# A four-layer transformer on one core: the order of a many-headed expert stage, a second routing's roots on ScalarE, and two moves at the seam of the first routing

## The chip, the cores and the metric

The kernel runs on one core of one Trainium2 chip. The metric is the device time of one execution in microseconds (us). A core has a matrix engine (PE; its weight loads are listed apart as PEld), a vector engine (DVE), a scalar engine (ACT, which evaluates functions from loaded tables), a general engine (POOL), and a queue that only starts transfers (SP). Each works through its own instruction queue in order, and they wait for each other on semaphores.

## The reference

`x` has 32 sequences of 256 rows with 128 features, 8192 rows in all. Four layers follow each other; each has an attention half and a feed-forward half, and each half is preceded by a layer norm and a modulation that depends on the sequence:

```
h = _layernorm(x, axis=-1) * (1 + ca) + sa
x = x + ga * attn(h)
h = _layernorm(x, axis=-1) * (1 + cb) + sb
x = x + gb * ffn(h)
```

The attention halves are a two-branch selective scan (layer 0), a local attention with Haar-level linear attention called "hale" (layer 1), an attention with phase windows (layer 2) and an attention over a latent of 32 (layer 3). The feed-forward halves that matter here are the first three:

```
# layer 0: a shared expert for every row, and 2 of 8 routed experts
shared = new_gelu(xf @ Wfc_s + bfc_s) @ Wproj_s + bproj_s
topk_p, topk_i = jax.lax.top_k(softmax(xf @ Wr), 2)     # then normalised
routed = sum over e of gate[:, e] * (new_gelu(xf @ Wfc[e] + bfc[e]) @ Wproj[e] + bproj[e])
# layer 1: 2 of 8 experts of 512 places each, filled in the order of the rows
logits = jax.nn.relu(x @ rw1 + rb1) @ rw2 + rb2
pos = jnp.cumsum(one_hot(ids), axis=0) - 1              # place of each row in its expert
disp[ids, pos] += x * (pos < CAP);  y = expert_out[ids, pos] * probs * keep
# layer 2: each of 8 heads (16 features) of each row picks 2 of 16 experts
h = x @ Wm + bm;  t = h.reshape(-1, 16);  w = softmax(t @ expert_emb)
hmid = gelu(einsum('td,edi->tei', t, W1) + b1);  eo = einsum('tei,eio->teo', hmid, W2) + b2
out = (sum of the two chosen eo, weighted by w) @ Wo + bo
```

The last feed-forward half quantizes its operands to FP4.

## The kernel before

`x` stays in the core's memory as 16 tiles of 512 rows, features on the partitions, rows along the free dimension. Eight stages run one after the other, each a method with its own pools of buffers (`pools`: a name and how many buffers it rotates through): `scan_layer`, `dense_moe` (L1009), `hale` (L1616), `capacity_moe` (L2076), `phase_attention`, `head_moe` (L2376), `latent_attention`, `fp4_mlp`. A buffer of a new stage lies in memory that an old stage's buffers had, and its first writer waits for their last readers.

**How the order is written.** Each stage fills an agenda: `put(t, f, ...)` enters a piece of work at step `t`, and the pieces are then called in order of `t`, those of one step in the order in which they were put. `mm` and `tr` (L398, L401) always pin the matmuls and transposes to that order, `act` (L405) pins ScalarE's where `strict_act` is set, and `nc.vector.on` pins VectorE's (by the wrapper `InOrder`, so that L310 is the profile's line for all of these). Whatever is not pinned is placed by the framework's scheduler. Matmul lines in the profile are L399, transposes L403, activations L406.

**dense_moe** (first routing). Tile `b` starts at step 4b: norm, rows `h`, logits, choice of 2 of 8 (`choose`), places, `scatter` (L1130: eight indirect transfers on POOL that put the tile's rows into the experts' regions in DRAM), gates (`route_gates`). 24 steps later `shared_part` (L1150, four pieces) computes the shared expert for this tile on PE and ACT and adds it to `x`. `route_totals` is at step 72, and 39 blocks of 512 routed rows follow, four steps each: `block_fetch` (weights `wts` and rows `dk` gathered by POOL), `block_turn` (four transposes `tp<-dk`), `block_hidden`, `block_out` (a copy `eo` by DVE, a store to `expert_rows` by SP). SP also issues the load of stage 7's weights, into the buffer that this stage's weights had, when the last reader of these is through.

**hale**. Its prelude makes constants: on POOL memsets of zeros and ones (`mts`, `vzb`, `vzl` at L1629 to L1632, `kvs` at L1639), on the other engines small weights. Then `hale_slots` runs an agenda whose first pieces, for each tile of 512, gather the routed rows that belong to it (`gather_rows`, L1294: two indirect transfers `got` on POOL for each of four row groups), sum them (`gather_sum`, `gy`) and add them to `x` (`gather_end`); norm and attention follow.

**capacity_moe** (second routing). Tile `b` starts at step 4b: `norm_stats` (transposes to PSUM, BATCH_NORM on DVE), `norm_apply` one step later, `norm_out` (rows `h`, transposed back), `router_hidden` (four matmuls and Relu), `router_sums` (logits `lT`, rows `ht`), `router_choice` (`choose`: two maxima with one-hots, `both`, then four running sums `past` and `seen`), `capacity_slots` (PE counts from `both` and `past`, DVE places, `scatter`). Only PE's order is pinned. With `newton` set, `norm_apply` takes 1/sqrt(v + eps) by integer shift and four Newton steps, all on DVE:

```
nc.vector.tensor_scalar(g, v.bitcast(I32), 1, None, ALU.arith_shift_right)
nc.vector.tensor_scalar(g, g, -1.0, float(0x5F3759DF), ALU.mult, ALU.add)
# four times: t = -0.5*y*y;  t = t*v;  y = (t + 1.5)*y
```

`rsqrt` (L413) is the other way: Ln and Exp on ACT and one refinement of four instructions on DVE. The weights and a zeroing of `disp` are issued as transfers at the start of the stage, part of them on ACT's queue.

**head_moe** (many-headed experts). A tile has 16 steps, one for each expert `e`: `moe_spread` (a transfer on SP that spreads the gate's row, `gb`), `moe_hidden` (four matmuls `S<-hm`, two Gelu of 128x1024 on ACT), and two steps later `moe_outputs` (four matmuls `po<-hid`, `ye = po * gb` on DVE, `acc += ye` on POOL). Between these the next tile is prepared: norm in three pieces (`moe_norm`, then Newton on DVE in two halves), rows (`moe_h`: transposes `tp<-ln_xn`, `h` on ACT), projection (`moe_heads`: `tp<-h,bigw`, `hm`), logits, choice, the exponential (`moe_exp`, with a table load before and after it), gates, `moe_turn`, `moe_bias`. All engines are pinned. In a step every `moe_hidden` is called first, then all other work. PSUM has three buffers for `S`, one for `po`, one for `tp`.

Of the kernel before, what the change touches and what calls it, by code (L numbers as in the profile page):

```python
# [30 lines left out]
P = 128  # L31
# [291 lines left out]
class Program:  # L323
# [129 lines left out]
    def norm_rows(self, src, small=None, tag="ln_xn"):  # L453

        nc = self.nc
        ps = self.ps("tp", (P, 4, P))
        for t in range(4):
            self.tr(ps[:, t, :], src[:, t * P : (t + 1) * P])
        xn = self.wk(tag, (P, 4, P))
        self.act(xn, ps, AF.Copy)  # L460
        st, mv, v = self.wk("ln_st", (P, 4, 6)), self.wk("ln_mv", (P, 4, 2)), self.wk("ln_v", (P, 4))
        for t in range(4):
            nc.vector.bn_stats(st[:, t, :], xn[:, t, :])
        for t in range(4):
            nc.vector.bn_aggr(mv[:, t, :], st[:, t, :])
        (small or nc.vector).tensor_scalar(v, mv[:, :, 1], 1e-5, None, ALU.add)
        return xn, mv, v

    def norm_place(self, xn, mv, v):
# [539 lines left out]
    def dense_moe(self, w):  # L1009
# [8 lines left out]
        with ExitStack() as ctx:  # L1018
# [19 lines left out]
            def put(t, f, *args):  # L1038
                agenda.setdefault(t, []).append((f, args))

            for b in range(NB):
                a = {"b": b}
                T = 4 * b
                put(T + 1, lambda a: a.update(xn=self.norm_apply(*a["st"])), a)
                put(T + 0, lambda a: a.update(st=self.norm_stats(self.x[a["b"]])), a)
                put(T + 3, lambda a: a.update(h=self.norm_out(a["xn"], self.ada_mods(0, 1, a["b"]), "h")), a)
                put(T + 5, self.route_logits, m, a)
                put(T + 10, self.route_slots, m, a)
                put(T + 13, self.route_gates, m, a)
                for i in range(4):  # L1050
                    put(T + 24 + i, self.shared_part, m, a, i)
            end = 4 * NB + 8
# [563 lines left out]
    def hale(self, w):  # L1616
        nc, c = self.nc, self.c
        BF = mybir.dt.bfloat16
        with ExitStack() as ctx:
# [8 lines left out]
            self.vzl = [keep.tile([P, 4, 16, 32], F, name=f"vzl{t}") for t in (0, 1)]  # L1628
            for t in self.mts + self.vzb + self.vzl:  # L1629
                nc.gpsimd.memset(t, 0.0)  # L1630
            for t in self.vzb + self.vzl:
                nc.gpsimd.memset(t[:, :, :, 8:16], 1.0)  # L1632
            self.identb = wk("identb", (P, P), BF)
# [4 lines left out]
            self.kvs = wk("kvs", (P, 5, SEQ))  # L1638
            nc.gpsimd.memset(self.kvs, 0.0)  # L1639
            self.kt = wk("kt", (P, 5, P))  # L1640
# [19 lines left out]
            self.gather = None  # L1660

    def hale_slots(self, w):

# [6 lines left out]

        tiles = {}
        for q in range(2 * NB):
            b, s = divmod(q, 2)
# [402 lines left out]
    def capacity_moe(self, w):  # L2076
# [3 lines left out]
        with ExitStack() as ctx:  # L2080
# [6 lines left out]
            self.pools(ctx, {"tp": 2, "hid": 3, "o": 1, "s": 2}, zero=1, ht=4, dk=4, hid=3, eo=3, h=3)  # L2087
            self.strict = self.newton = True
            zero = self.wk("zero", (P, 8 * P))
# [11 lines left out]
            def put(t, f, *args):  # L2101
                agenda.setdefault(t, []).append((f, args))

            for b in range(NB):
                a = {"b": b}
                T = 4 * b
                put(T + 1, lambda a: a.update(xn=self.norm_apply(*a["st"])), a)
                put(T + 0, lambda a: a.update(st=self.norm_stats(self.x[a["b"]])), a)
# [15 lines left out]
            for t in sorted(agenda):  # L2124
                for f, args in agenda[t]:
                    f(*args)
            self.strict = self.newton = False
            self.gather = {"eo": eo, "rows": 8 * CAP}
# [247 lines left out]
    def head_moe(self, w):  # L2376
# [5 lines left out]
        with ExitStack() as ctx:  # L2382
            w = self.load_pieces(ctx, "s5", [(x, None) for x in ("Wm", "bm", "emb", "b2", "b1", "w1", "w2", "Wo", "bo")])
            self.pools(ctx, {"S": 3, "po": 1, "tp": 1}, hid=6, gb=8, ye=3, hm=3, ln_xn=1)
            self.strict = self.strict_act = nc.vector.on = True
# [5 lines left out]
            for b in range(NB):  # L2391
                a = {"b": b}
                T = 16 * b
                put(T - 32, lambda a=a: self.moe_norm(a))
                for t in (-31, -30):
                    put(T + t, lambda a=a: next(a["norm"]))
                put(T - 28, lambda a=a: self.moe_h(a))
                put(T - 27, lambda a=a: self.moe_heads(w, a))
                put(T - 24, lambda a=a: self.moe_logits(w, a))
# [7 lines left out]
                for e in range(16):  # L2407
                    put(T + e - 3, lambda a=a, e=e: self.moe_spread(a, e))
                    put(T + e, (lambda a=a, e=e: self.moe_hidden(w, a, e), None))
                    put(T + e + 2, lambda a=a, e=e: self.moe_outputs(w, a, e))  # L2410
                put(T + 22, lambda a=a: self.moe_end(w, a))
            for t in sorted(agenda):
                works = agenda[t]
                for work in works:
                    if isinstance(work, tuple):
                        work[0]()
                for work in works:
                    if not isinstance(work, tuple):
                        work()
            self.strict = self.strict_act = nc.vector.on = False  # L2420
# [451 lines left out]
```

## Time and profile before

The kernel before took 6519.52 us (median of four runs, 6490.41 to 6537.06). One execution was profiled:

| | |
|---|---|
| profiled execution | 6520.15 us |
| its span | 6518.3 us, 132602 instructions |
| mean granted PE clock | 0.94 of full speed |
| busy: PE, PEld | 5750.6 us (88%), 3278.6 us (50%) |
| busy: DVE, ACT, POOL | 4205.6 (65%), 3472.7 (53%), 2855.7 (44%) |
| dense_moe | about 1055 to 1634 us of the span |
| hale | 1634 to 3683 |
| capacity_moe | 3683 to about 4042 |
| head_moe | about 4760 to 5520 |

A line of the timeline gives the start, the time from start to end, the engine, the code line, the operation, what it writes `<-` what it reads, and in brackets the idle time of the engine before it with what ended it. A line of the waits gives the waiting engine and what it was about to do, the instruction that it waited for, then the sum, the number and the longest of these waits. A line of the windows gives busy time and instructions of each engine, the granted PE clock, the share of the DMA engines that was busy, and the bytes moved. Busy shares over the whole span mix stages with different limits, so each edit is looked at in its own stretch.

### The profile page before, as it was taken

To read this page: it belongs to the slowest core of one execution; us is meant where nothing else is said; L and a number is where in the kernel's file an instruction comes from. 1 tells how busy PE (TensorE), PEld (TensorE's weight loads), DVE (VectorE), ACT (ScalarE), POOL (GpSimd) and SP (SyncE) were. 2 spreads that over 40 slices of the span, in tenths; PEclk is the share of its full clock that TensorE was granted. 3 is DMA by queue.
4 is the path that set the end of the run, shared out by engine and by line. 5 is a ranking of instruction groups with operands and counts; after the bars stand their busy time and mean duration, and the time that the engine had idled before them with its cause. 6 is when DMAs were issued, how large, how long until landed. Compare 5 with 4: busy or idle time off the path is not lost. (4 is left out here: it accounts for less than half of the span.)

```text
span 6518.3 us, 132602 instructions
## 1 busy us (share of the span) xinstructions
PE 5750.6 (88%) x54369; PEld 3278.6 (50%) x54369; DVE 4205.6 (65%) x9329; ACT 3472.7 (53%) x5045; POOL 2855.7 (44%) x3202
## 2 busy tenths in 40 slices
PE   6888886999899999999999776999979998999987
PEld 4666664466455555555555433455522222455544
DVE  4777776611466666666665562888767774677678
ACT  5888884333344444444444331444458887555532
POOL 4565553565444544444444353444334545222200
PEclk7999997999899999999999877999989999999988
DMA  2110111145000000000000101111034443000010
GB/s 63 42 43 35 37 42 38 48 118 125 16 6 5 7 6 5 6 6 5 7 3 2 48 1 36 24 29 29 24 82 90 92 91 75 14 20 20 19 35 30
DMA packets 175875, 232.17 MB, mean 36 GB/s; under 512 B 46567, under 2 KB 95967, under 8 KB 175010
## 3 DMA queue, kind: packets, MB, share of 16 engines
q1 hardware_dynamic: 124880, 126.50, 7.6%
q0 software_dynamic: 26992, 56.62, 3.7%
q10 hardware_dynamic: 23394, 40.58, 1.7%
q8 instruction: 427, 7.00, 0.5%
q14 instruction: 182, 1.49, 0.1%
HBM read 88.21 MB, written 74.97 MB: 25 GB/s over the span
## 5 line engine op out<-in xcount | busy, mean ns | idle before, releaser
L310 DVE TENSOR_REDUCE mt<-S 128x4 f32<-128x1024 f32 (+2 forms) x768 | 755.0, 998 | 534.0 <-PE S L399 530.6
L1471 ACT ACTIVATE E<-S 128x1024 f32<-128x1024 f32 x448 | 457.8, 1022 | 426.6 <-PE S L399 384.7
L910 DVE TENSOR_TENSOR_SCAN hs<-decay,dB 128x512 f32<-128x512 f32 x512 | 583.2, 1204 | 153.1 <-PE dB L399 113.8
L1962 POOL TENSOR_SCALAR_AFFINE_SELECT E<-E 128x1024 f32<-128x1024 f32 x320 | 348.7, 1092 | 584.3 <-ACT E L1961 583.9
L406 ACT ACTIVATE hid<-S,bigw 128x1024 f32<-128x1024 f32 x512 | 537.2, 1111 | 121.6 <-PE S L399 121.2
L310 DVE TENSOR_TENSOR E<-S,cst 128x1024 f32<-128x1024 f32 x320 | 391.1, 1222 | 289.3 <-PE S L399 289.2
L399 PE MATMUL S<-qa,kx 32*128 32x256 f32 x4096 | 510.9, 371 | 12.0 <-DVE mt L310 11.5
L399 PE MATMUL S<-kx,q 32*128 32x512 f32 (+1 forms) x2048 | 509.4, 591 | 3.0 <-POOL kx L1607 2.7
L2509 POOL TENSOR_TENSOR acc<-acc,ye 128x512 f32<-128x512 f32 x256 | 344.4, 1345 | 359.2 <-DVE ye L310 316.2
L1961 ACT COPY E<-S 128x1024 f32<-128x1024 f32 x320 | 323.5, 1011 | 325.3 <-PE S L399 313.5
L399 PE MATMUL S<-qG,f 32*128 32x512 f32 x2560 | 367.6, 644 | 47.4 <-DVE E L310 47.4
L399 PEld LDWEIGHTS S<-qa,kx 32*128 32x128 f32 x4096 | 325.9, 185 | 97.2 <-DVE mt L310 64.4
L403 PE MATMUL hT<-cst,hs 128*128 128x128 f32 x2048 | 298.8, 292 | 72.0 <-ACT hsT L406 68.1
L399 PE MATMUL S<-hm,bigw 32*128 32x512 f32 x2048 | 336.8, 649 | 24.9 <-ACT hid L406 24.9
L406 ACT ACTIVATE decay<-dl,A 128x510 f32<-128x510 f32 x512 | 338.5, 712 | 0.0
L406 ACT ACTIVATE hsT<-hT 128x1024 f32<-128x1024 f32 x256 | 259.7, 1015 | 122.3 <-PE hT L403 122.0
L399 PE MATMUL po<-hid,bigw 128*32 128x512 f32 x2048 | 277.9, 615 | 30.4 <-DVE ye L310 30.4
L403 PEld LDWEIGHTS hT<-cst,hs 128*128 128x128 f32 x2048 | 235.3, 148 | 124.7 <-ACT hsT L406 107.7
L1837 ACT ACTIVATE E<-S 128x768 f32<-128x768 f32 (+1 forms) x192 | 169.0, 880 | 237.7 <-PE S L399 237.5
L310 DVE TENSOR_TENSOR ye<-po,gb 128x512 f32<-128x512 f32 x256 | 175.9, 687 | 173.8 <-PE po L399 104.5
L399 PE MATMUL po<-E,vz 128*32 128x256 f32 x4096 | 287.1, 364 | 0.3 <-ACT oc L1491 0.2
L399 PE MATMUL po<-E,vzl 128*32 128x128 f32 x8192 | 276.8, 276 | 0.0
(540 smaller groups left out, 12985.4 us busy)
## 6 DMA issues: line engine op xcount, KB each, us to landing
gb<-gT SPq DMA_DIRECT2D x256, 256.0 KB
regions<-zeros ACTq DMA_DIRECT2D x16, 2048.0 KB
rx<-far SPq DMA_DIRECT2D x64, 256.0 KB
expert_rows<-eo SPq DMA_DIRECT2D x39, 256.0 KB
xin<-in_x SPq DMA_DIRECT2D x16, 256.0 KB
out<-out SPq DMA_DIRECT2D x16, 256.0 KB
xTd<-xT SPq DMA_DIRECT2D x15, 256.0 KB
xT<-xTd SPq DMA_DIRECT2D x15, 256.0 KB
```

The lines of the kernel that those rows point to most:

```text
L310: return lambda *args, **kw: self.tc.keep_in_program_order(op(*args, **kw))
L399: return self.tc.keep_in_program_order(self.nc.tensor.matmul(out, lhsT, rhs, start=start, stop=stop, **kw))
L403: return self.tc.keep_in_program_order(self.nc.tensor.transpose(out, in_, self.c.ident[:k, :k]))
L406: ins = self.nc.scalar.activation(*args, **kw)
L910: nc.vector.tensor_tensor_scan(hs[:, :, n], decay, dB[:, :, n], 0.0, ALU.mult, ALU.add)
L1471: nc.scalar.activation(e, src, AF.Exp, scale=scale)
L1837: nc.scalar.activation(e, src, AF.Exp, scale=1.0 / math.sqrt(8))
L1961: nc.scalar.copy(e, src)
L1962: nc.gpsimd.affine_select(e, e, [[0, 8], [1, P]], ALU.is_ge, 0.0, base=0, channel_multiplier=-1)
L2509: nc.gpsimd.tensor_tensor(a["acc"], a["acc"], ye, ALU.add)
```

## The change

Four edits. (A) In `dense_moe` the shared parts of tiles 9, 10 and 11 are put at the steps behind the last expert block. (B) In `hale` the memsets leave the prelude and become a piece of work, `hale_zeros`, at step -47 of the side agenda, where on POOL they stand behind the first tile's eight gathers. (C) In `capacity_moe` the norm's root is taken by Ln and Exp on ACT with one refinement on DVE, and the normalisation itself by four Identity activations that read PSUM with a scale and a bias (`norm_turned`); a preload of the Ln and Exp table is added at the stage's start, and `newton` is not set. (D) In `head_moe` the norm of a tile is put 16 steps earlier, for which `ln_xn` gets a second buffer; rows go from 28 to 31 steps ahead, the projection from 27 to 29, so that they stand on both sides of the exponential of the tile before (14 steps ahead of its own tile, that is step 2 of the 16); and in step 4 the outputs of expert 2 are called before the hidden part of expert 4. The instruction counts of all other stages and their order stay as they were.

```diff
+    def norm_turned(self, ps, mv, v):
+        nc = self.nc
+        rs, shift = self.wk("ln_rs", (P, 4)), self.wk("ln_m", (P, 4))
+        self.rsqrt(rs, v, "ln")
+        nc.vector.scalar_tensor_tensor(shift, mv[:, :, 0], -1.0, rs, ALU.mult, ALU.mult)
+        xn = self.wk("ln_xn", (P, 4, P))
+        for n in range(4):
+            self.act(xn[:, n, :], ps[:, n, :], AF.Identity, bias=shift[:, n : n + 1], scale=rs[:, n : n + 1])
+        return xn
...
 (dense_moe)
+                last = 4 * (8 + blocks + b + 7) if 9 <= b < 12 else T + 24
                 for i in range(4):
-                    put(T + 24 + i, self.shared_part, m, a, i)
+                    put(last + i, self.shared_part, m, a, i)
...
 (hale)
-            for t in self.mts + self.vzb + self.vzl:
-                nc.gpsimd.memset(t, 0.0)
-            for t in self.vzb + self.vzl:
-                nc.gpsimd.memset(t[:, :, :, 8:16], 1.0)
...
-            nc.gpsimd.memset(self.kvs, 0.0)
...
+    def hale_zeros(self):
+        nc = self.nc
+        for t in self.mts + self.vzb + self.vzl + [self.kvs]:
+            nc.gpsimd.memset(t, 0.0)
+        for t in self.vzb + self.vzl:
+            nc.gpsimd.memset(t[:, :, :, 8:16], 1.0)
...
 (hale_slots)
+        put(side, -47, self.hale_zeros)
...
 (capacity_moe)
-            self.strict = self.newton = True
+            self.strict = True
+            self.use_ln_exp()
...
-                put(T + 1, lambda a: a.update(xn=self.norm_apply(*a["st"])), a)
+                put(T + 1, lambda a: a.update(xn=self.norm_turned(*a["st"])), a)
...
-            self.strict = self.newton = False
+            self.strict = False
...
 (head_moe)
-            self.pools(ctx, {"S": 3, "po": 1, "tp": 1}, hid=6, gb=8, ye=3, hm=3, ln_xn=1)
+            self.pools(ctx, {"S": 3, "po": 1, "tp": 1}, hid=6, gb=8, ye=3, hm=3, ln_xn=2)
...
-                put(T - 32, lambda a=a: self.moe_norm(a))
-                for t in (-31, -30):
+                put(T - 48, lambda a=a: self.moe_norm(a))
+                for t in (-47, -46):
                     put(T + t, lambda a=a: next(a["norm"]))
-                put(T - 28, lambda a=a: self.moe_h(a))
-                put(T - 27, lambda a=a: self.moe_heads(w, a))
+                put(T - 31, lambda a=a: self.moe_h(a))
+                put(T - 29, lambda a=a: self.moe_heads(w, a))
...
-                    put(T + e, (lambda a=a, e=e: self.moe_hidden(w, a, e), None))
-                    put(T + e + 2, lambda a=a, e=e: self.moe_outputs(w, a, e))
+                    early = 1 if e == 4 else 0
+                    put(T + e, (lambda a=a, e=e: self.moe_hidden(w, a, e), early))
+                    early = 0 if e == 2 else None
+                    put(T + e + 2, (lambda a=a, e=e: self.moe_outputs(w, a, e), early))
...
-                works = agenda[t]
-                for work in works:
-                    if isinstance(work, tuple):
-                        work[0]()
-                for work in works:
-                    if not isinstance(work, tuple):
-                        work()
+                works = [x if isinstance(x, tuple) else (x, None) for x in agenda[t]]
+                for place in (0, 1, None):
+                    for work, at in works:
+                        if at == place:
+                            work()
```

## The prediction

> **What bounds the kernel now.** I read the page's busy shares first: PE 88% of the span, DVE 65%, ACT 53%, POOL 44%. The edits touch three places, so I cut the span there and asked for the windows, then for the timeline, the waits and the groups inside each. Times are us from the span's start.
>
> ```profile
> core 0: us, PE busy (x) PEld busy (x) DVE busy (x) ACT busy (x) POOL busy (x), PEclk, DMA share, GB/s
> 1245.00:1302.00 57.00, 54.90 (x168) 25.94 (x167) 34.06 (x160) 19.36 (x33) 37.67 (x39) 0.97 0.19 60
> 1302.00:1327.00 25.00, 16.82 (x30) 6.25 (x28) 1.63 (x4) 2.99 (x5) 14.04 (x15) 0.73 0.19 55
> 1327.00:1633.00 306.00, 304.70 (x1712) 213.35 (x1712) 53.51 (x79) 107.21 (x156) 175.07 (x176) 1.00 0.49 127
> 1633.00:1658.00 25.00, 3.95 (x20) 2.59 (x20) 7.90 (x20) 2.77 (x3) 19.16 (x23) 0.63 0.13 35
> 3750.00:3900.00 150.00, 109.48 (x390) 56.64 (x390) 98.02 (x685) 55.97 (x97) 81.66 (x84) 0.74 0.02 1
> 4890.00:5379.00 489.00, 451.00 (x2974) 130.47 (x2974) 365.23 (x684) 401.96 (x398) 243.36 (x178) 0.98 0.40 91
> ```
>
> The fourth line is the 39 expert blocks of the first routing: PE has no idle there, so whatever is put behind them is paid in full. The fifth is the seam to hale: PE idle, POOL busy. Its timeline on POOL:
>
> ```profile
> 1635.78 1.32 POOL L1630 MEMSET mt<- 128x256 f32 x4 [21.41 <-DMA expert_rows<-eo]
> ...
> 1643.81 1.16 POOL L1639 MEMSET kvs<- 128x1280 f32 x1
> 1645.13 1.01 POOL L1299 DMA_INDIRECT got<-expert_rows,back  x1 [0.16 <-issue]
> ```
>
> The first gather waits behind 9.2 us of memsets. On PE, a tile's shared part and the only stall ahead of the blocks:
>
> ```profile
> 1288.88 3.60 PE L399 MATMUL hid<-h,w 128*128 128x512 f32 x8
> 1292.41 1.12 PE L399 MATMUL o<-gT,w 9*128 9x512 f32 x2
> 1293.46 3.70 PE L399 MATMUL o<-hid,w 128*128 128x512 f32 x8
> ...
> 1315.68 2.08 PE L399 MATMUL hid<-h,w 128*128 128x512 f32 x2 [7.83 <-ACT hid L406]
> ...
> 1319.69 6.52 PE L399 MATMUL o<-hid,w 128*128 128x512 f32 x8
> 1326.04 0.60 PE L403 MATMUL tp<-cst,dk 128*128 128x128 f32 x4
> ```
>
> In the second routing (waits of tiles 3754 to 3896; ten tiles, 14.17 each between their first BATCH_NORM) no engine is full. A chain through DVE's choice, `s` on PE and the scatters bounds it:
>
> ```profile
> POOL disp L1134 <- ACT lT L406: 53.2, 11, 10.4
> ACT lT L406 <- PE s L399: 43.4, 10, 4.8
> PEld s L399 <- DVE past L1096: 15.9, 10, 2.3
> PE s L399 <- DVE past L1096: 14.6, 10, 2.2
> DVE past L1096 <- DVE past L1096: 7.1, 9, 1.2
> ```
>
> The last line is odd: dependent sums of 0.17 us with holes of about 0.55 between them. In head_moe (waits of 4890 to 5379) PE and ACT alternate; a tile takes 45.58 (from table load to table load, 5066.66 to 5112.24):
>
> ```profile
> PEld po L399 <- DVE ye L310: 101.4, 102, 1.3
> ACT hid L406 <- PE S L399: 80.9, 103, 1.1
> PEld S L399 <- ACT hid L406: 70.9, 66, 2.5
> ```
>
> **Part A, shared parts of tiles 9 to 11 behind the blocks.** Three times 8.12 (1288.88 to 1297.00) is 24.4 us. Put at the end they are paid: **+24.4**, on PE, for the first gather waits for the last shared matmul (its tile takes that pool's memory). ACT and the x updates run under PE as before. Ahead of the blocks PE had those 24.4 us between 1245 and 1327. What then bounds the start is POOL: a tile's 8 scatters are 10.2 us (8 x 1.28), against 13.6 from tile to tile now (b12 at 1247.08, b13 at 1260.70). Two periods at 10.2 bring the fetch forward by 7.4 at least; PE at most by 24.4, with the 1.1 and part of the 7.83 idle perhaps 27. Replayed with the rows' durations, b15's fetch is at 1288, its rows land about 1300, and the four shared parts left end about 1297 to 1301 instead of 1326. The stall (ACT's hid waits 12.7 for nothing shown while fetches fill the queues) may recur. I take **-20** (12 to 27; POOL alone 7.4), nearer the PE end since PE is 96% busy from 1245 to 1302. SP's 560 KB load for a later stage waits for the last reader of these weights, so it moves from 1326 to the end, beside the first gathers: 0 to +2, **+1**.
>
> The row for PE idle: after the 7.83 us stall the same eight matmuls took 6.52 against 3.70. The Trainium skill, "TensorE: Matmul & The Clock Gate", Part 1, says the clock halves after one idle window of about 3.4 us and needs a busy one to return. It speaks against this part: with less PE cover, any wait over 3.4 us makes the remaining shared parts run at half rate, by the rule up to 8 us more for each; A would then give about -12 instead of -20, which is the end of my range anyway.
>
> **Part B, memsets behind the first gathers.** The last matmul ends at 1632.63, the eo copy at 1633.35, its store lands at 1635.77, the memsets end at 1644.97: the first gather is 12.5 after PE. Afterwards copy and store lie under the shared parts, and the memsets stand between gathers 8 and 9 on POOL: **-12.4**. Queued behind them are tile 1's gathers; their first sum is 32 steps on, and the local keys that read the zeros are later than the first tile's x (1657.8). If that cover is gone, up to 9.2 returns. A+B = -20 + 24.4 + 1 - 12.4 = **-7** (-15 to +6).
>
> **Part C, the second routing's roots.** Gone from DVE for each tile: 14 Newton instructions (0.16 each in the group rows, one every 0.11 while two chains interleave) and four 128x128 normalisations (1.35, 3814.97 to 3816.32); added there, 5 small ones. Added on ACT: Ln and Exp (0.205 by the 128x4 row) and four 128x128 Identity; head_moe's 128x512 Copy is 0.60, which bounds four from below, and the 128x128 scaling elsewhere on ACT is about 0.41 to 0.49, so 2.0 to 2.4 in all. ACT is busy 5.3 of 14.2, so it covers them. Ln waits for DVE's variance with three hidden activations queued behind it; the variance is there at 3811.6, when the first of them ends at 3811.8. In the tile at 3811: `lg` at 3812.45, thirteen dependent steps at 0.20 give `both` at 3816.0 rather than 3816.7 and the last sum at 3816.8 rather than 3820.1 if the holes vanish: period 11.0 (POOL's floor 10.2), 3.2 less. But in every tile the holes sum to about 2.2. I keep two thirds (1.5) since nothing in the edit touches them except the neighbours that stood in between: 12.5, 1.7 less. Fifteen periods: -25.5. Against that, at the start ACT's queue issues weight and zero DMAs till 3702.63; Newton ran on DVE under that, Ln can't: +3.8 to +5, taken 4.5, with one table load of 1.28 inside. C = **-21** (15 x 3.2 - 4.5 gives -43.5; all holes kept, -10.5).
>
> Table loads here: load, exponential, load take 3.24 (5066.66 to 5069.90), their own durations. The Trainium skill, "ScalarE: Activation LUTs", "What ACT_TABLE_LOAD costs", counts a drain of 1.38 more for each. By that page C would be -19.6; these rows show no such drain.
>
> **Part D, head_moe.** The norm keeps its phase in the period (16 steps earlier), needing a second ln_xn buffer; so only the order moves: rows `h` (1.04 on ACT, 0.66 on PE) ahead of the exponential, the projection (1.07 on PE, 0.74 on DVE) just behind it, and in step 4 outputs 2 before hidden 4. No DMA moves. Now PE idles 1.65 at 5071.06 behind ACT's load, exponential, load, and ACT idles 1.00 at 5078.06 and 1.14 at 5081.32 for S. Replayed: the exponential ends 1.04 later, the projection fills PE's 1.65, outputs 2 end by 5072.2 with their ye buffer free at 5071.1, hidden 4 at 5072.7 is in time for ACT at 5073.0, and ACT runs without a hole to 5079.3; step 7's S is at 5078.8 rather than 5080.1, step 5's outputs at 5080.3 rather than 5081.5. Queued behind the new wait (outputs 2 for ye) on PE is hidden 4, and ACT waits for that. That is 1.2 a tile, 16 tiles, **-19**. Bounds: PE's idle in a tile is at most 3.7 (1.7 + 2.0 by its group rows), of which two thirds is the most I see; if outputs 2 wait for ye behind Newton (4.1 us of DVE) nothing is left: -40 to 0.
>
> **Sum.** -7 - 21 - 19 = -47 on the profiled execution (6520.15; span 6518.3), that is 6473. The median of before is 6519.5, 0.6 below it.
>
> **Rivals.** (1) The holes stay and the scatters or ACT's late start eat the rest: C = +4.5 to -10, total 6484 to 6499. For: holes in every tile; against: the startup chain on DVE at 3686 runs dependent steps at 0.20 with none. (2) The start of the blocks is set by POOL alone: A is -7.4, A+B +5.6, total 6486. For: 12.7 us of unexplained ACT wait there. (3) Outputs 2 block hidden 4 and D is 0: 6492. For: PE's po waits for ye 101 us in 489. (4) Slower: without Newton between them, eight dependent choice steps each get the 0.55 hole of the `past` rows: 4.4 less 0.9 saved is +3.5 a tile, C = +57, total 6551; it outweighs A, B and D from +1.4 a tile. Against: the holes stand only at the chain's end. (5) Holes vanish, D is 2 a tile: -7 - 43.5 - 32, 6438.
>
> **How the numbers follow.** Forecast 0.40; (1) 0.14; (2) 0.08; (3) 0.12; (4) 0.12; (5) 0.14. Half a per cent, what a measurement here can tell, is 33 us: 6487 and 6552. Faster: nearly all of the forecast and (5), a third of (1) and (2): 0.61. Slower: half of (4) and a little: 0.08. Same 0.31. The range leaves the lower part of (5) and the upper half of (4) out: 6436 to 6535; the forecast's own is 6450 to 6490.
>
> **What will show it.** Right: blocks start near 1305, the first gather within a microsecond or two of the last shared matmul, second-routing period 11 to 12.5 with `lT` waits gone from POOL, head_moe period about 44.4 with PE's 1.65 gone. Wrong: holes on all choice steps, blocks still starting after 1318, `ye` waits grown.

## The result and the profile after

After: 6529.84 us (median of 52 runs, 6517.42 to 6542.24) against 6518.21 for the kernel before (median of 78 runs, 6489.22 to 6545.19). The ratio is 1.0019, 95% interval 1.0013 to 1.0025: 0.2% slower, where 0.7% faster was forecast. The profiled execution took 6534.37 us (span 6532.7, mean PE clock 0.94).

Where the time went, by events that both traces have (us from the span's start):

| event | before | after | difference so far |
|---|---|---|---|
| tile 12's first scatter in the first routing | 1247.1 | 1251.3 | +4.2 |
| first block's transposes `tp<-dk` | 1326.04 | 1333.66 | +7.6 |
| last block's last matmul | 1632.62 | 1640.24 | +7.6 |
| first gather of hale | 1645.13 | 1665.35 | +20.2 |
| first tile's `x` in hale | 1657.80 | 1686.51 | +28.7 |
| first BATCH_NORM of the second routing | 3684.39 | 3705.74 | +21.4 |
| first `tp<-dk` of the second routing | 3949.81 | 3975.62 | +25.8 |
| first exponential of head_moe | 4764.36 | 4790.33 | +26.0 |
| last exponential of head_moe | 5439.87 | 5447.25 | +7.4 |
| end | 6518.31 | 6532.66 | +14.4 |

The first row is no effect of the change: +4.0 of it stand already at the first scatter of the routing (1077.93 and 1081.95), ahead of every edit. Behind it only head_moe gained, and hale's later tiles. Windows of the kernel after, the same stretches as before (us, then busy time and instructions of each engine, granted clock, DMA):

```profile
core 0: us, PE busy (x) PEld busy (x) DVE busy (x) ACT busy (x) POOL busy (x), PEclk, DMA share, GB/s
1245.00:1302.00 57.00, 39.11 (x120) 21.58 (x119) 32.53 (x162) 10.51 (x19) 36.55 (x40) 0.71 0.13 42
1302.00:1327.00 25.00, 11.79 (x22) 3.78 (x20) 0.88 (x2) 2.36 (x4) 17.44 (x18) 0.71 0.35 104
1327.00:1633.00 306.00, 304.76 (x1677) 210.66 (x1677) 53.25 (x78) 107.03 (x157) 175.72 (x176) 0.99 0.47 125
1633.00:1658.00 25.00, 25.00 (x91) 13.00 (x90) 3.13 (x6) 7.96 (x12) 0.00 (x0) 1.00 0.08 22
3750.00:3900.00 150.00, 95.75 (x357) 47.28 (x357) 68.12 (x490) 62.52 (x144) 82.81 (x85) 0.76 0.02 4
```

The work moved by A left PE: 54.90 us became 39.11 in the first line. But the blocks did not start earlier, and the granted clock fell from 0.97 to 0.71. In the stretch from 1633 to 1658 the last block and then the shared parts fill PE, while POOL does nothing at all.

The stall ahead of the blocks, in the timeline after:

```profile
1307.35 2.74 PE L399 MATMUL hid<-h,w 128*128 128x512 f32 x6
...
1319.71 0.88 DVE L570 SCALAR_TENSOR_TENSOR x<-o,mods,x 128x256 f32<-128x256 f32 x2 [19.40 <-remote]
...
1322.56 0.69 ACT L406 ACTIVATE hid<-hid,w 128x512 f32<-128x512 f32 x1 [16.23 <-remote]
1323.30 2.07 PE L399 MATMUL hid<-h,w 128*128 128x512 f32 x2 [13.21 <-issue]
...
1333.66 0.60 PE L403 MATMUL tp<-cst,dk 128*128 128x128 f32 x4
```

PE's six matmuls end by 1310.1, yet ACT, which by its semaphores waits only for PE and for its own earlier work, starts 12.5 us later, and PE then waits 13.21 where it waited 7.83 before. `remote` means that the view finds no instruction whose end released the wait. By the trace's semaphore records the increments of PE's semaphore, for which ACT waits, come at 1313.38, 1316.18, 1319.68 and 1322.48, the last of them 12.4 us after the modelled end of the matmuls; ACT starts at 1322.56. POOL issues the gathers of `dk` one after the other all this time.

The seam to hale, in the same view:

```profile
1665.35 1.00 POOL L1313 DMA_INDIRECT got<-expert_rows,back  x1 [43.35 <-PE o L399]
...
1676.53 1.08 POOL L1674 MEMSET mt<- 128x256 f32 x4
1676.86 8.67 DVE L310 TENSOR_SCALAR gy<-got,pair 128x128 f32<-128x128 f32 x1 [0.90 <-DMA got<-expert_rows,back]
...
1684.44 1.01 POOL L1676 MEMSET vzl<- 128x512 f32 x2
1686.51 0.87 DVE L570 SCALAR_TENSOR_TENSOR x<-tp,mods,x 128x256 f32<-128x256 f32 x2 [0.57 <-PE tp L403]
```

The gather does follow the last shared matmul directly. But the `gy` of the first tile's fourth pair takes 8.67 us: it lasts as long as the memsets. In the kernel before it took 0.29:

```profile
1655.53 0.29 DVE L310 TENSOR_SCALAR gy<-got,pair 128x128 f32<-128x128 f32 x1 [0.85 <-DMA got<-expert_rows,back]
```

The second routing's waits after (3763 to 3921: engine, what it was about to do, what it waited for, total us, times, longest) and its tile starts on DVE:

```profile
POOL disp L1148 <- ACT lT L406: 46.4, 5, 11.7
PEld hid L399 <- ACT hid L406: 44.8, 5, 11.8
DVE ln_st L435 <- remote: 44.5, 4, 12.6
```

```profile
3777.26 0.89 DVE L435 BATCH_NORM_STATS2 ln_st<-tp 128x6 f32<-128x128 f32 x4 [1.17 <-PE tp L403]
3788.27 0.89 DVE L435 BATCH_NORM_STATS2 ln_st<-tp 128x6 f32<-128x128 f32 x4
3808.51 0.89 DVE L435 BATCH_NORM_STATS2 ln_st<-tp 128x6 f32<-128x128 f32 x4 [11.15 <-remote]
```

The eleven waits of POOL for `lT` (53.2 us in 142 us before) have become five that cost nearly as much together (46.4 in 158). The holes between the `past` sums are gone, a tile takes 11.0 when it goes well (3777.26 to 3788.27), and then one stands for 11 us. There too the signal is late: PE's last matmul ends at 3801.03 and its increment comes at 3808.49, when DVE goes on. Head_moe's waits after, and the stretch around its exponential:

```profile
PEld po L399 <- DVE ye L310: 115.5, 104, 2.3
PEld S L399 <- ACT hid L406: 75.4, 98, 1.2
ACT hid L406 <- PE S L399: 74.0, 108, 1.3
```

```profile
4951.54 1.12 PE L399 MATMUL tp<-h,bigw 128*128 128x512 f32 x2
4951.75 0.63 ACT L406 ACTIVATE ex<-ex 128x512 f32<-128x512 f32 x1
4952.39 1.28 ACT L406 ACT_TABLE_LOAD   x1
4954.13 1.06 PE L399 MATMUL po<-hid,bigw 128*32 128x512 f32 x8 [1.47 <-DVE ye L310]
```

The projection stands behind ACT's exponential, and ACT's hole after it is shorter (0.55 at 4956.36, before 1.00 at 5078.06 and 1.14 at 5081.32). Where it stands PE had this wait before:

```profile
5071.06 1.13 PE L399 MATMUL S<-hm,bigw 32*128 32x512 f32 x4 [1.65 <-ACT hid L406]
```

Nine periods from exponential to exponential take 407.65 us (4906.48 to 5314.13) against 419.61 before (4928.09 to 5347.70).

### The profile page after: what moved, and what is told of

Its sections match the earlier page's. It is cut to its first block, busy times and chain, and to the rows that moved or that the text cites. A ratio compares the mean times of both kernels' runs of the same rounds, so it can differ in the third digit from the quotient of the medians.

```text
span 6532.7 us, 132442 instructions
## 1 busy us (share of the span) xinstructions
PE 5748.6 (88%) x54369; PEld 3280.8 (50%) x54369; DVE 4173.7 (64%) x9121; ACT 3497.6 (54%) x5142; POOL 2862.3 (44%) x3202
## 5 line engine op out<-in xcount | busy, mean ns | idle before, releaser
L399 PE MATMUL po<-hid,bigw 128*32 128x512 f32 x2048 | 274.0, 607 | 44.4 <-DVE ye L310 44.4
```

The lines of the kernel that those rows point to most:

```text
L399: return self.tc.keep_in_program_order(self.nc.tensor.matmul(out, lhsT, rhs, start=start, stop=stop, **kw))
```

## The experiments

The experiments ran in three groups, each on a chip of its own. The unchanged kernel took 6455.26 us on the first (24 runs, 6445 to 6465), 6453.38 on the second (16 runs, 6446 to 6467) and 6518.25 on the third (16 runs, 6505 to 6530), which is the time of the result. All ratios below are to the kernel before on the same chip.

### Each part alone (first chip)

A alone has the new place of the shared parts and nothing else; B alone has `hale_zeros` on POOL, C alone `norm_turned`, D alone the order of head_moe. Some lines of each, the rest being as in the whole change:

```diff
# A
+                last = 4 * (8 + blocks + b + 7) if 9 <= b < 12 else T + 24
-                    put(T + 24 + i, self.shared_part, m, a, i)
+                    put(last + i, self.shared_part, m, a, i)
...
# B
...
+        put(side, -47, self.hale_zeros)
...
# C
...
-                put(T + 1, lambda a: a.update(xn=self.norm_apply(*a["st"])), a)
+                put(T + 1, lambda a: a.update(xn=self.norm_turned(*a["st"])), a)
...
# D
...
-                put(T - 28, lambda a=a: self.moe_h(a))
-                put(T - 27, lambda a=a: self.moe_heads(w, a))
+                put(T - 31, lambda a=a: self.moe_h(a))
+                put(T - 29, lambda a=a: self.moe_heads(w, a))
...
```

> The change in dense_moe alone (shared parts of tiles 9 to 11 behind the blocks; memsets stay in hale's prelude). Theory 1 (back-to-back indirect transfers on POOL hold up the other engines' signals, so work taken out ahead of the blocks brings nothing): first block 3 to 8 us later than before, then 24.4 us of shared matmuls; the memsets run on POOL under them, so the first gather is 16 to 20 us later than before and the time 16 to 20 us longer (ratio 1.0025 to 1.003). Rival (the memsets can't start under the shared parts, and moving them is what kept the loss down): 28 to 32 us longer. Rival (the prediction's step, 20 us won ahead of the blocks): 4 us longer or less.

> The memsets moved behind the first gathers, alone. If the seam's 9.2 us of memsets and the 3 us of copy and store ahead of them were the price: the copy and store stay on the path (the gather reads those rows), so 9 us are won: ratio 0.9986. Rival (the cover is gone: the second tile's gathers or the first local keys wait for the memsets): 0 to 4 us won, with a wait on POOL's memsets or on got in hale's first 60 us.

> The second routing's roots alone. Theory 1 (eight scatters of a tile hold up signals whatever the rest does): mean distance of the tiles stays at 13.6 to 14.2 us, in fast tiles of 10 to 12 us and stalls of 8 to 12 us after 16 scatters in a row; with the late start of ACT the time is 2 to 6 us longer (ratio 1.0003 to 1.0009). Rival (what was lost in the whole change in this stage was a chance of that execution): 15 to 25 us shorter (0.9962 to 0.9977).

> The change in head_moe alone. From the tables of the whole change (first to last exponential 18.6 us shorter, 2 us given back at the stage's end): 15 to 19 us shorter, ratio 0.9971 to 0.9977; distance of exponentials 45.3 in place of 46.5 in the steady part. Rival (the 7 us that the whole change was longer behind the last exponential belong to this part): 9 to 12 us shorter, ratio 0.9982 to 0.9986.

| part | median | ratio, 95% interval | us by the ratio | forecast |
|---|---|---|---|---|
| A | 6476.42 | 1.0035 [1.0021, 1.0048] | +23 | +5.4 (-20 + 24.4 + 1) |
| B | 6458.33 | 1.0006 [0.9997, 1.0015] | +4 | -12.4 beside A; 9.2 of it are the memsets |
| C | 6434.33 | 0.9969 [0.9957, 0.9981] | -20 | -21 |
| D | 6436.94 | 0.9977 [0.9968, 0.9986] | -15 | -19 |

C and D are what the forecast said, A and B are not. Of what was expected before these runs, theory 1 failed both in A (the first block comes earlier, not later) and in C (no stalls), C's rival and D's figure came out, and B's 9 us did not come. The sum, -8, is not the +12 of the result, though, so something differs between the occasions; the whole kernels were run again for that (next part).

**A.** Its price is read best from tile 12's first scatter to the first block. Windows of just that stretch, of D alone and then of A alone:

```profile
1239.50:1305.50 66.00, 65.22 (x190) 29.98 (x189) 33.02 (x146) 22.55 (x37) 46.91 (x48) 0.97 0.21 66
```

```profile
1244.70:1300.40 55.70, 47.19 (x137) 23.24 (x135) 29.52 (x140) 14.62 (x25) 43.62 (x43) 0.82 0.22 73
```

The stretch is 10.3 shorter, not 24.4. PE's busy time falls by 18.0 only, since at a granted clock of 0.82 instead of 0.97 what remains takes 6.4 longer (busy time times clock, 63.3 and 38.7, falls by 24.6); and PE's idle time grows from 0.8 to 8.5. What it waits for is the choice of the last tiles, in the timeline of A alone:

```profile
1252.79 1.62 PE L403 MATMUL tp<-cst,ln_xn 128*128 128x128 f32 x4 [3.41 <-DVE rt_o L608]
...
1261.18 1.01 PE L403 MATMUL tp<-cst,gate 128*9 128x128 f32 x4 [2.15 <-DVE rt_m L599]
1263.40 0.61 PE L399 MATMUL s<-both,cst 128*128 128x32 f32 x2 [1.20 <-DVE both L1091]
```

Behind the blocks, in A alone:

```profile
1641.37 1.07 POOL L1631 MEMSET mt<- 128x256 f32 x4 [42.72 <-PE o L399]
...
1650.71 1.01 POOL L1300 DMA_INDIRECT got<-expert_rows,back  x1 [0.16 <-issue]
```

The memsets too wait for the last shared matmul. From the last block's matmul to the first tile's `x` of hale it takes 46.44 us rather than 25.19: +21.3, the 24.4 paid less the copy and store (3.1) that now lie under the shared parts. Together +11 of the 23. Part of the rest comes later in hale: from that `x` to the second routing 2023.9 us, against 2018.2 and 2019.1 in C and D alone on the same chip. Why is open, and that stretch varies by 4 between kernels that are alike there.

**B.** The timeline of B alone:

```profile
1619.32 1.00 POOL L1299 DMA_INDIRECT got<-expert_rows,back  x1 [22.05 <-DMA expert_rows<-eo]
...
1630.45 1.08 POOL L1660 MEMSET mt<- 128x256 f32 x4
1630.72 8.73 DVE L310 TENSOR_SCALAR gy<-got,pair 128x128 f32<-128x128 f32 x1 [0.92 <-DMA got<-expert_rows,back]
...
1638.35 1.01 POOL L1662 MEMSET vzl<- 128x512 f32 x2
```

The first gather is 3.8 after the last block's matmul (1615.52) rather than 12.5. Then the memsets reach DVE's fourth `gy` and hold it for 8.73 us, so that the first tile's `x` is 24.90 after that matmul rather than 25.19. Nothing is gained.

**C.** Scatters run back to back, and POOL sets the period. Tile starts on DVE in C alone:

```profile
3762.19 0.89 DVE L435 BATCH_NORM_STATS2 ln_st<-tp 128x6 f32<-128x128 f32 x4
3772.28 0.88 DVE L435 BATCH_NORM_STATS2 ln_st<-tp 128x6 f32<-128x128 f32 x4
3782.60 0.88 DVE L435 BATCH_NORM_STATS2 ln_st<-tp 128x6 f32<-128x128 f32 x4
```

The tiles shown are 10.2 apart, at the floor of POOL's 8 x 1.28 (the earlier ones, ahead of POOL, 8.5 to 9.1), and the 128 scatters take 163.3 us.

### The whole again, and two variants (second chip)

`cd` is C and D without A and B. `d_rows` is D with the new places of rows and projection, but without the outputs of expert 2 ahead of the hidden part of expert 4:

```diff
-                    early = 1 if e == 4 else 0
+                    early = 0
-                    early = 0 if e == 2 else None
+                    early = None
```

> The kernel before, unchanged, for its trace beside the next runs. Theory 2 (whether POOL's runs of indirect transfers hold up the other engines' signals is a condition of the chip, not of the kernel): where the time is near 6455 us, the sums of the choice follow each other at 0.20 us without holes, the second routing's tiles are 11.5 to 12.5 us apart in place of 14.17 and the first block starts near 1305 in place of 1326; where it is near 6518, as in the first profile. Theory 1 as first stated (the holds belong to the kernel's own runs of transfers): holes and 14.17 at either time.

> The changed kernel, unchanged. Theory 2: where the kernel before takes about 6455 us, the sum of the single parts holds: 21 for the shared parts, 0 to 3 for the memsets, -21 for the roots, -18 for head_moe, so 13 to 18 us shorter (ratio 0.9972 to 0.9980), with 16 and more scatters in a row and no stall; where it takes about 6518, 12 us longer as first measured (1.0019). Theory 1: 12 us longer in both.

> The roots and head_moe without the two moves at the first routing. Theory 2, chip without held signals: 36 to 39 us shorter (ratio 0.9940 to 0.9944); chip with held signals: 12 to 14 us shorter (0.9978 to 0.9982), since the roots give nothing there. Rival (the parts interfere, so that the whole is worth less than the sum): under 30 us shorter where the kernel before takes 6455.

> Head_moe with the norm ahead, rows and projection around the exponential, but hidden 4 before outputs 2 as it was. If the rows and the projection carry the gain: 14 to 18 us shorter, as with the whole part. If the outputs first in step 4 carry it (rows before the exponential only move ACT's work): 0 to 6 us shorter.

| kernel | median | ratio, 95% interval | us by the ratio |
|---|---|---|---|
| before again (one run) | 6453.09 | | |
| after again | 6432.89 | 0.9968 [0.9955, 0.9980] | -21 |
| C + D | 6412.38 | 0.9939 [0.9926, 0.9953] | -39 |
| D without outputs first | 6438.87 | 0.9981 [0.9972, 0.9990] | -12 |

The same change that cost 0.2% in the result gains 0.3% here. So the sign of the result depends on the chip (or the occasion). C + D gains 39, as expected, and A + B take back half of it. `d_rows` is 2 to 3 us short of D alone with intervals that overlap, and from the first to the last exponential it isn't short at all (657.9 us, D alone 660.1): the rows and the projection carry D, and the outputs' order is worth little or nothing.

What differs is seen in the unchanged kernel. Windows of the second routing from its first scatter to its last, in the result's trace and then here:

```profile
3722.00:3945.00 223.00, 141.94 (x500) 72.91 (x498) 130.13 (x905) 71.95 (x126) 123.95 (x128) 0.71 0.02 4
```

```profile
3699.00:3883.00 184.00, 141.66 (x500) 71.33 (x498) 130.49 (x905) 72.20 (x126) 123.89 (x128) 0.77 0.03 4
```

The engines do the same work in the same busy time, in 39 us less. From tile 12's first scatter to the first block it is 66.2 us rather than 79.0. The stall of 7.83 us and the holes between the `past` sums, which the prediction took for properties of the kernel, are not there (23 of the 64 sums had such a hole in the result's trace, here none). The same code in the timeline of the kernel before, in the result's trace and then on the second chip:

```profile
3817.86 0.17 DVE L1096 TENSOR_TENSOR past<-past,both 128x8 f32<-128x8 f32 x1 [0.54 <-DVE rt_p L623]
3818.58 0.17 DVE L1096 TENSOR_TENSOR past<-past,both 128x8 f32<-128x8 f32 x1 [0.48 <-DVE rt_p L624]
3819.30 0.17 DVE L1096 TENSOR_TENSOR past<-past,both 128x8 f32<-128x8 f32 x1 [0.55 <-DVE past L1096]
```

```profile
3813.51 0.17 DVE L1096 TENSOR_TENSOR past<-past,both 128x8 f32<-128x8 f32 x1
3813.71 0.37 DVE L1096 TENSOR_TENSOR past<-past,both 128x8 f32<-128x8 f32 x2
```

The trace's semaphore records tell why. Outside of POOL's runs of indirect transfers, an increment by DVE or ACT arrives 0.01 us after its instruction's end (means 0.03 or less, on every chip). Mean delay of DVE's increments that fall 2 to 10 us into such a run, and the share of them later than 0.2 us:

| kernel | mean, us | share over 0.2 us |
|---|---|---|
| before, after (the result) | 0.49, 0.56 | 0.59, 0.59 |
| all eight kernels of the first two chips | 0.01 | 0.00 |
| zeros by ACT, C + D + zeros by ACT (third chip) | 0.42, 0.53 | 0.55, 0.60 |
| half the scatters, before and after (third chip) | 0.27, 0.33 | 0.39, 0.41 |

ACT's are held longer, 1.22 and 1.76 on the mean in the result's two traces, with single ones over 10 us, and PE's 0.86 and 0.82; it is PE's for which ACT and DVE stood in the stalls of 13.21 and 11.15. An engine that waits for such an increment is shown as waiting for `remote` or `issue`. On the first two chips nothing is held even 163 us into a run.

### Late signals, and fewer of them (third chip)

For B the zeros and ones are written by ACT instead of POOL, at the same place in the order; `cd_act` is C, D and this:

```diff
+    def hale_zeros(self):
...
+                nc.scalar.activation(t[:, at : at + n], self.zeros[:, :n], AF.Copy)
...
+                nc.scalar.activation(t[:, k, :, 8:16], self.c.ones.rearrange("p (h c) -> p h c", c=8), AF.Copy)
```

In `half_before` and `half_after`, the kernels before and after, `scatter` puts only the first choice's rows into place, in both routings, and leaves out the second choice's:

```diff
-            for k in (0, 1):
+            for k in (0,):
```

> As the memsets moved behind the first gathers, but the zeros and ones are written by ACT (31 copies of up to 128x512, some 16 us by its rows, while it is idle) and POOL has only the gathers. Theory 3 (POOL's memsets hold DVE's sum of the fourth pair of gathers for 8.7 us, the same time that they no longer stand ahead of the gathers): the sum takes 0.3 us again, the first x is 8 to 9 us earlier than before and the time 6 to 9 us shorter (ratio 0.9986 to 0.9991). Rival (the fourth pair was late for another reason, its transfer or its semaphore): the sum still waits about 9 us and the time is that of before.

> The roots, head_moe, and the zeros by ACT, without the shared parts moved. If the three add up: 41 us of the two and 6 to 9 more, ratio 0.9925 to 0.9931. If ACT's copies push the first norms of hale: as without them, 0.9939.

> The kernel before with only the first choice of each row scattered, in both routings (four indirect transfers for a tile in place of eight; the second choice's rows are left out, so experts work on zeros in their places). Theory 2: POOL no longer sets any distance. Second routing 9 to 10 us from tile to tile; the scatters of the first routing end with its tiles and not 16 in a row.

> The changed kernel with only the first choice of each row scattered, in both routings (second choice left out as in the other). If POOL's scatters were what took the gain of the shared parts ahead of the blocks: the first block starts 15 to 24 us earlier than in the other kernel with half the scatters. If the fetch of weights and rows sets it anyway: 0 to 8 us earlier. Second routing 8.5 to 9 us from tile to tile; where signals are held, no stalls of 8 us and more are left, since no 16 scatters stand in a row.

| kernel | median | ratio, 95% interval | us by the ratio |
|---|---|---|---|
| B, zeros by ACT | 6509.57 | 0.9991 [0.9981, 1.0002] | -6 |
| C + D + zeros by ACT | 6495.91 | 0.9967 [0.9955, 0.9979] | -22 |
| half the scatters, before (one run) | 6444.89 | | |
| half the scatters, after (one run) | 6402.06 | | -43 to the line above |

**Zeros by ACT.** The sums of the first tile are no longer held:

```profile
1644.51 4.25 ACT L1664 ACTIVATE vzl<-zeros 128x512 f32<-128x512 f32 x8
...
1646.37 0.30 DVE L310 TENSOR_SCALAR gy<-got,pair 128x128 f32<-128x128 f32 x1 [0.79 <-DMA got<-expert_rows,back]
```

and the first `x` comes 17.5 us after the last block's matmul rather than 25.2. So 7.7 of the 12.4 are there to be had when the writer is not POOL. In the time it is -6 with an interval that includes 1, so the trace shows the gain and the time alone does not. With C and D it is less than either branch of the expectation, since C gains nothing here: the scatters take 224.5 us.

**Half the scatters.** The same edit of 12 us loss gains 43 on a chip that holds signals, once POOL's runs are half as long. That is one run of each (the kernel before spread over 25 us on this chip), and part of the 43 is that POOL no longer bounds the second routing, whose tiles are 8.4 apart at the end. Three intervals in which the two parts can be compared, in us:

| | tile 12's first scatter to first block | second routing: first BATCH_NORM to first scatter | first to last scatter |
|---|---|---|---|
| before, after (the result) | 79.0, 82.3 | 37.9, 40.3 | 223.3, 225.3 |
| before again, after again (second chip) | 66.2, 56.0 | 37.6, 40.5 | 184.3, 163.3 |
| half: before, after (third chip) | 66.1, 55.8 | 37.6, 40.3 | 157.2, 130.0 |
| D alone, A alone; C alone (first chip) | 66.0, 55.7 | C: 40.0 | C: 163.3 |

With half the scatters A gains the same 10 as where signals come at once (and POOL, with half its work gone, doesn't change that: it is PE's waits and clock that set it); the expectation had 15 to 24 or 0 to 8. C gains 27 in the scatters' stretch rather than losing 2. Windows of the second routing, half before and then half after, from about the first scatter to the last:

```profile
3705.00:3862.00 157.00, 124.64 (x499) 61.94 (x497) 125.78 (x904) 71.16 (x125) 62.17 (x64) 0.87 0.02 3
```

```profile
3711.00:3840.00 129.00, 109.96 (x498) 55.32 (x496) 100.29 (x730) 88.10 (x203) 61.36 (x64) 0.95 0.02 3
```

DVE's busy time falls by 25.5 us, the stretch by 28. With the runs half as long, the stretch ahead of the blocks takes in both kernels what it takes where signals come at once, the late increments are fewer (table of delays), and in the kernel before none of the 64 sums has a hole any more, where B with zeros by ACT, on the same chip with all its scatters, has 20. That the length of POOL's runs of transfers sets what the late signals cost on such a chip is thereby shown; what in the chip does the holding is not.

**Better than both.** C + D is the fastest where signals come at once (0.9939). Where they are held, C + D + zeros by ACT beats both kernels (0.9967); on the first two chips it was not run, nor was C + D without the zeros on the third.

## Why the prediction was wrong

Between the forecast of -47 and the +14.4 of the two traces, A ahead of the blocks makes 23 us (-20 became +3.4), C 25 (-21 became +4.4) and the seam 8 (the 24.4, 1 and -12.4 became +21.1). D came out.

**D, right.** -19 was forecast; the trace of the result gives -18.6 from the first to the last exponential, and the part alone -15 [-21, -9]. The 16 tiles gain 1.3 each (nine periods 419.61 to 407.65) where 1.2 was forecast. The named period of 44.4 was wrong as a figure: 45.58 was one of the shorter tiles before (others take 47.1), and 45.27 is what nearly all have now. Outputs 2 do wait for `ye` (1.47 us at 4954.13, where PE's 1.65 had been), and the waits for `ye` grew from 101.4 to 115.5, so the third rival's mechanism is there at a small size. The replay's third move, outputs 2 before hidden 4, was not needed (`d_rows`).

**C, right in size where signals come at once, the first rival where they are held.** The forecast was a start later by 4.5 and 25.5 gained over the periods. On the second chip the start is later by 2.9 and the scatters gain 21.0. That the time fits is in part luck: the forecast was worked out for tiles 14.17 apart with holes, and there were none here, the tiles going from about 11.9 to between 8.5 and 10.9. In the result the start is later by 2.4 and the scatters lose 2.0: +4.4, the upper end of the first rival. The step that failed is "I keep two thirds (1.5) since nothing in the edit touches them": the holes did go, all of them, and other waits of the same origin took their place, fewer and longer (11.15 and 12.6 rather than 0.55). One sum on the way was off too: thirteen steps of 0.20 from 3812.45 put `both` at 3815.1 and not at 3816.0, and then POOL's floor of 10.2 and not 11.0 is the period without holes, which is what C alone shows. The table loads still stand back to back with no drain between them (4951.75 to 4953.69), so the page's figure for C, -19.6, isn't supported by the rows; the time of C, -20 [-28, -12], can't tell the two apart.

**A ahead of the blocks, wrong by half at best.** "I take -20 ... nearer the PE end since PE is 96% busy" failed. Where signals come at once the gain is 10.3: 24.4 less 6.4 for the lower clock and 7.7 for waits that the shared parts had covered. The replay had the order right and left both out of the sum. In the result it is a loss of 3.4: PE idles 30.3 us between tile 12's scatter and the first block, against 9.9 before, at a clock of 0.69 against 0.89; the stall whose return was named and priced at nothing grew from 7.83 to 13.21. The second rival gave nearly the right size (-7.4, which is the sum over three periods and not two) for the wrong reason, since POOL with half its work leaves the stretch at 55.8. In A alone the trace's clock records stand at half for 20.5 us of the stretch, from 1249.6 to 1270.1, beginning with the wait of 3.41 that ends at 1252.79; in D alone for 3.4 us. The Trainium skill, "TensorE: Matmul & The Clock Gate", Part 1, which the prediction weighed, gave an estimate of -12. The halved clock at the wait of 3.41 agrees with its warning that a PE which idles for about 3.4 us loses half its clock; no run here separates the clock from the waits further than the sum above.

**A behind the blocks, right.** 24.4 were to be paid, and 21.3 are, since the last copy and store lie under them; the prediction gave these 3.1 to B.

**B, wrong.** The gather moved as forecast: in the result it comes 25.1 after the last block's matmul, where 24.4 + 0.7 is the shared parts alone, and A + B is +12.6 there against +12.0 forecast. But "the memsets stand between gathers 8 and 9 on POOL" looked only for work queued behind them on POOL. DVE's sum ran beside them and stood still for 8.67, so at the first `x` A + B is +21.1. The trace of before had the hint: under the memsets DVE's `sw` of 128x4 took 1.02 and 1.37 us, and without them 0.23 and 0.28. The Trainium skill, "SBUF — State Buffer", "Who interferes with whom", has the rule: DVE's tensor_scalar can enter a mode that takes the port pair it shares with GpSimd, and then one of the two stands still for the other's whole instruction, while ACT has ports of its own. The 0.30 beside ACT's writes fit that, and the two TENSOR_SCALAR of 128x4 in A alone, which end 0.03 after the one memset beside them. The 8.73 us go beyond it: the wait lasted for thirteen instructions of POOL and not for one, and the measurement decides. The rule speaks against part B, and the prediction left it out.

**What stays open.** In the result hale's later tiles gave back 7.4 us (+28.7 to +21.4), and 7.0 were lost after the last exponential of head_moe: 1.6 up to the stage's last `S` matmul, as in D alone, and 5.4 behind it. From there to the end it takes 1015.8 us in the result's kernel after, 1015.7 on the second chip and 1015.2 in `d_rows`, but 1010.5 in D alone and 1009.3 with half the scatters, where the code is the same, so it may be no effect of the change. The runs don't decide it. Nor do they tell whether the late signals belong to a chip or to an occasion, since each chip was used at one time only.

## What to carry to other kernels

A row of waits that names no instruction (`remote`, or an engine that starts long after all its inputs have ended) is a price by itself: look at what POOL is issuing at that time, and where it is a run of indirect transfers, count on the wait to move rather than to vanish when the work around it is shortened. Moving work off an engine that is 96% busy gains only down to the next chain, so work out that chain first and take its figure as the forecast. And when POOL writes constants, look at what DVE does beside it, not only at what is queued behind.

## What the runs showed of the hardware

- The same kernel took 6453 to 6455 us on two chips and 6518 on a third, by ranges that don't overlap (highest 6467, lowest 6505). The traces differ in the delay of semaphore increments during POOL's runs of indirect transfers: 0.01 us on the two, with all scatters 0.4 to 0.6 on the mean for DVE, 0.7 to 1.1 for PE, and over 10 for single ones of ACT on the other. It isn't the moved bytes: in the second routing the DMA engines move 1 GB/s from 3750 to 3900 us, and DVE's increments are late there by 0.35 on the mean.
- Thirteen memsets by POOL in a row held one TENSOR_SCALAR of DVE, 0.28 us by itself, for 8.73, though POOL changes instruction twelve times in between. In A alone TENSOR_REDUCE and RECIPROCAL of 128x1 ran beside the same memsets in their usual 0.14 to 0.16, and TENSOR_SCALAR of 128x4 took 0.82 and 1.45, to the end of the one memset beside it. Why that of 128x128 was held through all of them no run shows.
